# Hadamard transform of the feed-forward input on GpSimd instead of in its weights, norm transposes without TensorE, three slots of keys and values

## The chip, the cores and the metric

The kernel runs on one core of a Trainium2 chip, in float32. A core has five engines that work side by side, each through its own queue of instructions in program order: TensorE (PE, matrix products into PSUM), VectorE (DVE), ScalarE (ACT), GpSimd (POOL) and SyncE (SP), which here issues nearly all DMA transfers. An instruction that waits holds up everything behind it in its queue. The metric is the device time of one execution in microseconds (us): the median of three runs before the change is 2125.62 (2123.35 to 2127.01).

## The reference

One transformer block with modulated norms, 4 sequences of 1024 tokens, 512 features, 16 query heads of 32 that share one key and one value head, and a feed-forward part of width 2048 whose input and inner activations pass a Walsh-Hadamard transform (`fwht`, normalized):

```python
mod = (silu(c) @ wmod).reshape(4, 6, 1, -1)       # sa, ca, ga, sb, cb, gb
ga, gb = sign(ga) * maximum(abs(ga), 0.25), sign(gb) * maximum(abs(gb), 0.25)
h = layernorm(x) * (1 + ca) + sa
x = x + ga * attention(h)                         # causal; q, k, v, o with biases
h = layernorm(x) * (1 + cb) + sb
# feed-forward of h:
u = fwht(h * SU_ug) / SCALE
up   = u @ W_up.T   * (Wscale_ug[:2048] * SCALE)
gate = u @ W_gate.T * (Wscale_ug[2048:] * SCALE)
d = fwht(silu(gate) * up * SU_dp) / SCALE
x = x + gb * (d @ W_down.T * (Wscale_dp * SCALE))
```

## The kernel before

The 4096 tokens form 8 blocks of 512 (two to a sequence), 16 halves of 256 and 32 token tiles of 128. The kernel does not write its instructions in a fixed order: each part (norms, projections, scores, exponentials, attention products, feed-forward, loads) is a generator that yields operations with a cost in microseconds, the keys it reads and writes, and conditions to wait for. A planner (`Flow`) keeps a clock for each engine from these costs, emits the operation that can begin first and, among those within 0.3 us on the same engine, the one of the lowest rank. So each engine's queue order is fixed when the kernel is built, out of the planned costs. The chip then runs each queue in that order and waits where real durations differ from planned ones.

*Attention.* `first_norms` loads a half (2 tiles), takes mean and variance on DVE, the inverse root on POOL (`rstd_op`), normalizes on DVE, and `norm_half` transposes it with eight 128x128 TensorE transposes (L300) into PSUM, from where ACT scales and shifts it into `hT` (L305). `fronts` makes keys, values and queries from `hT` (L271). A `Unit` is one tile of queries by 8 or 16 heads. For each, `scores` (PE, L420), `minima` (DVE, L441), `exps` (ACT, L463), `scales` (ACT, and POOL for every other head of block 0, L487 and L484), `turns` (DVE 32x32 transposes, L502) and `attend` (PE, L529) follow, with two units in flight in the buffer `p`. Keys and values of one whole sequence are kept, so the first block of the next sequence waits until the last one has been attended. `finish` folds the heads (L563) and multiplies by the output weights (L271). `add` multiplies by the gate `ga` and adds `x` on POOL (L593, L594), stores the tile to DRAM (`x2_d`, called x_d in the trace) and takes its statistics.

*Feed-forward.* `second_norms` loads tiles from `x2_d` again, normalizes them, and `norm_half` turns them on TensorE into `bt`. `gate_up` computes gate and up with a two-by-two block scheme of seven products (L905, weights `wa` and `wb` streamed from DRAM), `copies`, `sums` and `multiply` work on them on ACT and DVE (L979, L992, L1008, L1013), and `down` multiplies by the down weights `wd` (L1043). `outputs` adds the result on DVE and POOL (L1070, L1075). A feed-forward block may start once `st.normed` says that all four of its tiles are in `bt` and the four sums T1 to T4 are made (L616). Ranks put attention ahead of `down` and `gate_up`, so the feed-forward of one block fills TensorE beside the attention of the next.

*Preparation.* The Hadamard transforms do not act on activations but on weights. `load_jobs` brings 18 jobs of 1 MB into three buffers in `p`: 6 parts of the modulation weights and 4 each of gate, up and down. `butterflies` does the outer steps on DVE and POOL (L763), `transforms` the inner 128-point transform as TensorE products (L788 to L795) with an ACT copy (L801), and `mixes` (L832) forms the sums of the block scheme, which are stored to `wa_d` and `wb_d`. `hand_over` waits until this is done, frees the buffers and lets `gate_up` begin.

All transfers of the feed-forward are issued on SP in the planned order, with 2 buffers for `wa` and `wb` and 3 for `wd`.

Of the kernel before, what the change touches and what calls it, by code (L numbers as in the profile page):

```python
# [9 lines left out]
F32 = mybir.dt.float32  # L10
# [150 lines left out]
def adaln_block(ctx, tc, x_d, small_d, const_d, wmod_d, qwT_d, kwT_d, vwT_d, vb_d, owT_d, ob_d,  # L161
# [16 lines left out]
    x2_d = dram.tile([B * S, D], F32, name="x2_d")  # L178
    wd_d = dram.tile([NFC, P, D], F32, name="wd_d")
    gates_d = dram.tile([2, B, D], F32, name="gates_d")  # L180
    rows = [slice(HD * j, HD * j + HD) for j in range(4)]

# [3 lines left out]
    xn = {"a": sb("xna", 2, D), "f": sb("xnf", 2, D)}  # L186
    xr, xo = sb("xr", 2, D), sb("xo", 2, D)
# [6 lines left out]
    cg, wgh, qbs = sb("cg", NFC), sb("wgh", NFC), sb("qbs", NDC)  # L194
    scT = sb("scT", NDC, HD)
    kT = sb("kT", S)
    vT = sb("vT", HB)
    vrep = sb("vrep", S // 32, HD)
# [7 lines left out]
    mv = {"a": sb("mva", 2, 2, 2), "f": sb("mvf", NBLK * NT, 2)}  # L206
    rstd = {"a": sb("rstda", 2, 2), "f": sb("rstdf", 2, 2)}
    PB = 8192
    p = sb("p", 2 * PB)
# [3 lines left out]
    oT = sb("oT", 4, H, 32)  # L213
    rden = sb("rden", 4, H)
    aT = sb("aT", NDC, P)
    ga, y, y2 = sb("ga", D), sb("y", 2, D), sb("y2", D)
# [46 lines left out]
    def bk(b):  # L263
        return ("bank", b)
# [21 lines left out]
    def norm_half(which, buf, means, rs, rkey, dst, dkey, scale, bias, need, free):  # L286

        x = xn[buf]
        for j in range(2):
            yield Op("DVE", 0.62, lambda: nc.vector.tensor_scalar(  # L290
                x[:, j, :], x[:, j, :], means[j], rs[:, j:j + 1], ALU.subtract, ALU.mult),
                [rkey], [("xn", buf, j)])
        yield free
        yield banks.have(2)
        bb = banks.take(2)

        def turn():
            for dc in range(NDC):
                for j in range(2):
                    nc.tensor.transpose(ps[:, bb[dc // 2], (dc % 2) * HB + j * P:][:, 0:P],  # L300
                                        x[:, j, dc * P:(dc + 1) * P], ident)
        yield Op("PE", 8 * 0.107 + 0.05, turn, [("xn", buf, 0), ("xn", buf, 1)],
                 [bk(b) for b in bb], mode="full")
        for dc in range(NDC):
            yield Op("ACT", act_cost(HB), lambda: nc.scalar.activation(  # L305
                dst(dc), ps[:, bb[dc // 2], (dc % 2) * HB:][:, 0:HB], AF.Identity,
                bias=bias[:, dc:dc + 1], scale=scale[:, dc:dc + 1]), [bk(bb[dc // 2])] + need, [dkey(dc)])
            if dc % 2:
                banks.give(bb[dc // 2])


    def first_norms(halves):
        for hh in halves:
            i, hf = divmod(hh, 2)
            b = i // BPB

            buf = "f" if hh == 1 else "a"
            x = xn[buf]
            yield lambda: st.fronts >= (hh - 1 if hh > 1 else 0)
            for j in range(2):  # L320
                r = hh * HB + j * P
                yield load(0.25, x[:, j, :], x_d[r:r + P, :], [("xn", buf, j)])
            m = mv["a"][:, hf]
            for j in range(2):
                yield stats_op("a", j, x[:, j, :], m[:, j, :], [("xn", buf, j)], ("mva", hf, j))
            rs = rstd["a"][:, hf, :]
            yield rstd_op(rs, m[:, :, 1], [("mva", hf, 0), ("mva", hf, 1)], ("rstda", hf))
            yield from norm_half("a", buf, [m[:, j, 0:1] for j in range(2)], rs, ("rstda", hf),
                                 lambda dc: hT[:, dc, :], lambda dc: "hT",
                                 modT[:, 1, :, b], modT[:, 0, :, b], ["mod0", "mod1"],  # L330
                                 lambda: st.fronts >= hh)
            st.first_normed = hh + 1

    def fronts(blocks):
        for i in blocks:
            b, t = divmod(i, BPB)
            for hf in range(2):
# [3 lines left out]
                yield lambda: t or st.attended_blocks >= i  # L341
# [37 lines left out]
    class Unit:  # L379
# [11 lines left out]

        def key(self, h):
            return ("p", self.base, h)

    units = []
    for i in range(NBLK):
        heads = 8 if i % BPB or i == 0 else 16
# [744 lines left out]
```

## Time and profile before

The profiled execution took 2121.98 us, of which the span of the program is 2120.1. It reads as follows ("busy" is the time in which an engine has an instruction running; a busy TensorE includes the modelled ends of pipelined products):

| stretch, us from the start | what runs | PE busy | DVE busy | ACT busy | POOL busy | DMA share |
|---|---|---|---|---|---|---|
| 0 to 50 | loads, first norms | 37.51 | 17.34 | 17.29 | 11.00 | 0.72 |
| 50 to 100 | preparation, block 0 of attention | 49.07 | 37.41 | 31.26 | 22.42 | 0.66 |
| 100 to 150 | the same | 45.96 | 42.61 | 31.90 | 36.67 | 0.89 |
| 150 to 200 | the same | 46.71 | 43.31 | 32.00 | 40.60 | 0.35 |
| 250 to 500 | feed-forward beside attention | 236.80 | 162.78 | 143.56 | 17.28 | 0.34 |
| 500 to 1000 | the same | 496.20 | 320.64 | 301.44 | 37.20 | 0.38 |
| 1000 to 1500 | the same | 496.60 | 317.50 | 295.78 | 41.20 | 0.39 |
| 1950 to 2120 | last feed-forward block | 158.71 | 54.63 | 28.67 | 8.50 | 0.46 |

The first gate and up product (L905) starts at 236.6 us; the last feed-forward block starts at 1958 us. The granted TensorE clock is 0.991 of full speed over the span.

### The profile page before, as it was taken

How to read it: one execution, taken by the hardware profiler on the slowest of the kernel's cores; microseconds unless marked ns; L12 is line 12 of the kernel's file. 1: busy time of each engine (PE TensorE's matmuls, PEld its weight loads, DVE VectorE, ACT ScalarE, POOL GpSimd, SP SyncE). 2: the span in 40 equal slices, each digit the busy share in tenths (PEclk: the TensorE clock that was granted, in tenths of full speed). 3: DMA queues.
4: the chain of work that ended last, by engine and by line, in shares of the span. 5: the costliest groups of instructions: out<-in, count | busy, mean ns of one | idle time of the engine just before them, and what ended most of it. 6: DMA issues, size and time to landing. Idle time of an engine off the chain costs nothing.

```text
span 2120.1 us, 41569 instructions
## 1 busy us (share of the span) xinstructions
PE 2056.1 (97%) x16884; PEld 1323.9 (62%) x16884; DVE 1315.7 (62%) x3057; ACT 1172.2 (55%) x2417; POOL 256.6 (12%) x224
## 2 busy tenths in 40 slices
PE   7999899989999999999999999999999999999998
PEld 4545566637766556666666656665766656664774
DVE  3788657774566777763566667763566667764331
ACT  3665556573756666654567565644757565553220
POOL 2467000100000100001100100001100100001000
PEclk9999899998999999999999999999999999999999
DMA  6773433332343434343433444334343444335443
GB/s 241 252 254 110 142 115 118 125 115 66 112 132 110 140 124 131 96 145 98 131 120 122 136 127 133 117 106 131 98 139 100 130 138 132 117 101 161 142 154 121
DMA packets 144599, 280.18 MB, mean 132 GB/s; under 512 B 14092, under 2 KB 44940, under 8 KB 144408
## 3 DMA queue, kind: packets, MB, share of 16 engines
q1 hardware_dynamic: 141384, 274.84, 40.4%
q8 instruction: 133, 2.18, 0.4%
q10 hardware_dynamic: 3024, 2.69, 0.4%
q14 instruction: 58, 0.48, 0.1%
HBM read 241.81 MB, written 35.67 MB: 131 GB/s over the span
## 4 chain that ended last, share of the span: by engine, by line
PE 89%; DVE 3%; issue 2%; DMA 2%; POOL 2%; ACT 1%; SPq 0%; POOLq 0%; ACTq 0%; DVEq 0%
PE ps L905 37%; PE ps L1043 20%; PE ps L271 11%; PE ps L529 9%; PE ps L420 7%; PE ps L563 1%; PE ps L300 1%; DVE p L441 1%; PE ps L794 1%; PE ps L795 1%; POOL p L484 1%; DVE p L502 1%; DMA p<-in_wgT 1%; DMA wd<-wd_d 1%; PE ps L788 0%
## 5 line engine op out<-in xcount | busy, mean ns | idle before, releaser
L905 PE MATMUL ps<-bt,wa 128*128 128x256 f32 x2560 | 607.0, 382 | 6.6 <-issue 4.2
L905 PEld LDWEIGHTS ps<-bt,wa 128*128 128x128 f32 x2560 | 483.5, 191 | 109.2 <-issue 29.2
L1043 PE MATMUL ps<-wd,g 128*128 128x512 f32 x1024 | 480.9, 603 | 6.7 <-DVE g L1018 3.9
L502 DVE STREAM_TRANSPOSE p<-p 128x256 f32<-128x256 f32 (+7 forms) x256 | 347.0, 1368 | 121.6 <-ACT p L487 111.3
L463 ACT ACTIVATE p<-p,nm 128x512 f32<-128x512 f32 (+7 forms) x512 | 390.9, 767 | 34.4 <-DVE nm L441 34.3
L487 ACT ACTIVATE p<-p,rden 128x640 f32<-128x640 f32 (+7 forms) x480 | 347.4, 783 | 25.0 <-DVE rden L467 24.9
L441 DVE CUSTOM_DVE_ANT_0 p<-ps,maskw 128x512 f32<-128x512 f32 (+3 forms) x512 | 277.2, 585 | 105.6 <-PE ps L420 105.1
L992 DVE TENSOR_TENSOR s<-ps,s 128x256 f32<-128x256 f32 x384 | 161.0, 420 | 274.7 <-PE ps L905 205.8
L1043 PEld LDWEIGHTS ps<-wd,g 128*128 128x128 f32 x1024 | 184.7, 190 | 219.0 <-issue 175.7
L905 PE MATMUL ps<-bt,wb 128*128 128x256 f32 x1024 | 271.5, 387 | 0.6 <-DVE s L992 0.5
L905 PEld LDWEIGHTS ps<-bt,wb 128*128 128x128 f32 x1024 | 187.6, 190 | 93.0 <-issue 51.2
L529 PE MATMUL ps<-p,vrep 32*32 32x256 f32 (+1 forms) x8256 | 196.3, 418 | 18.5 <-DVE p L502 7.3
L1008 ACT ACTIVATE th<-s,wgh 128x512 f32<-128x512 f32 x128 | 92.4, 722 | 202.0 <-DVE g L1018 158.0
L420 PE MATMUL ps<-kT,qT 32*128 32x512 f32 (+3 forms) x1536 | 188.6, 533 | 2.9 <-DVE nm L441 2.3
L983 ACT COPY s<-ps 128x256 f32<-128x256 f32 x128 | 47.6, 372 | 254.7 <-PE ps L905 254.7
L593 POOL TENSOR_TENSOR y<-y,ga 128x512 f32<-128x512 f32 x32 | 40.7, 1272 | 1156.6 <-DVE y L576 1088.4
L529 PEld LDWEIGHTS ps<-p,vrep 32*32 32x32 f32 x8256 | 123.4, 104 | 90.5 <-issue 33.7
L441 DVE CUSTOM_DVE_ANT_0 p<-ps,maskw,nm 128x128 f32<-128x128 f32 (+3 forms) x256 | 129.4, 546 | 20.2 <-PE ps L420 20.0
L420 PEld LDWEIGHTS ps<-kT,qT 32*128 32x128 f32 x1536 | 69.5, 183 | 97.8 <-issue 67.4
L539 ACT COPY oT<-ps 128x256 f32<-128x256 f32 (+1 forms) x208 | 75.8, 430 | 90.9 <-PE ps L529 89.7
L271 PE MATMUL ps<-ow,aT 128*128 128x512 f32 x256 | 115.4, 593 | 1.8 <-ACT aT L567 1.8
L271 PE MATMUL ps<-hT,qw 128*128 128x256 f32 x512 | 116.4, 384 | 0.3 <-DVE nm L441 0.3
(99 smaller groups left out, 1585.0 us busy)
## 6 DMA issues: line engine op xcount, KB each, us to landing
wa<-wa_d SPq DMA_DIRECT2D x128, 640.0 KB, 4.7
wd<-wd_d SPq DMA_DIRECT2D x256, 256.0 KB, 2.6
wb<-wb_d SPq DMA_DIRECT2D x128, 256.0 KB, 2.6
xr<-in_x SPq DMA_DIRECT2D x32, 256.0 KB, 2.8
x_d<-xr SPq DMA_DIRECT2D x32, 256.0 KB, 2.1
xnf<-x_d SPq DMA_DIRECT2D x32, 256.0 KB, 3.7
xo<-x_d SPq DMA_DIRECT2D x32, 256.0 KB, 3.9
out<-xo SPq DMA_DIRECT2D x32, 256.0 KB, 2.3
```

What stands on the lines that cost most here:

```text
L271: nc.tensor.matmul(out, l, r, start=(k == 0), stop=(k == len(pairs) - 1))
L420: nc.tensor.matmul(ps[:, bb[j], 0:n], qT[r, c, u.ql * P:(u.ql + 1) * P], kT[r, kb * 512:kb * 512 + n], start=True, stop=True)
L441: yield Op("DVE", 0.245 + 0.00103 * n, lambda: nc.vector.tensor_tensor_reduce(o, ps[:, bb[j], 0:n], m, -1.0, nm[:, slot, 0, j:j + 1] if kb ...
L463: yield Op("ACT", act_cost(u.kmax) + 0.19, lambda: nc.scalar.activation(e, e, AF.Exp, bias=nm[:, slot, u.t, j:j + 1], scale=-1.0, accum_ou ...
L487: yield Op("ACT", act_cost(u.kmax), lambda: nc.scalar.activation(e, e, AF.Copy, scale=r), [("rden", ds, c)], [u.key(h)])
L502: yield Op("DVE", 0.135 + 0.00105 * 2 * u.kmax, lambda: nc.vector.transpose(e, e), [], [u.key(h), u.key(h + 1)])
L529: nc.tensor.matmul(ps[rows[c], bb[g], 0:w], vrep[rows[g], 4 * kt + c, :], pv[rows[g], :, k:k + 32], start=(kt == 0), stop=(kt == nkt - 1))
L539: yield Op("ACT", act_cost(w), lambda: nc.scalar.copy(oT[:, g, u.h0:u.h0 + u.heads, :], ps[:, bb[g], 0:w].rearrange("p (h q) -> p h q", q= ...
L905: nc.tensor.matmul(o, ff[name][:, k % 2, j, c * P:(c + 1) * P], bt[:, t, c, :], start=start and c == 0, stop=stop and c == 1, skip_group_c ...
L992: yield Op("DVE", 0.43, lambda: nc.vector.tensor_add(s[:, j, :], ps[:, bank, half * HB:(half + 1) * HB], s[:, j, :]), [bk(bank)], [sk[j]])
L1008: yield Op("ACT", act_cost(512), lambda: nc.scalar.activation(th, s[:, 0:2, :], AF.Tanh, scale=wgh[:, f:f + 1]), [sk[0], sk[1]], ["th"])
L1043: nc.tensor.matmul(ps[:, acc[j], :], g[:, j * P:(j + 1) * P], ff["wd"][:, m % NWD, :], start=(f == 0), stop=(f == NFC - 1))
```

## The change

The Hadamard transform of the feed-forward's input now acts on the activations. The new `transformed` takes each tile after `add`, normalizes and modulates it with two DVE instructions (rows `sc2r`, `bi2r` spread over the partitions), does nine steps of sums and differences of neighbours on GpSimd (18 instructions of 128x256), transposes 32x32 squares on DVE, and writes the tile with four DMAs (`turn`) to a transposed copy in DRAM, `xTf_d`. `inputs` loads it into `bt` (`turned`). The norms of attention from the third half on take the same way through `xTa_d`, with ACT modulating `hT` in place; the first two halves keep the TensorE transposes. Gate and up weights need no transform: `mixes` works on the raw weights, `butterflies` and `transforms` keep the down weights only. Keys and values have three slots of a block in place of one sequence. `oT` holds 8 heads, so `finish` folds in two steps. On POOL, one head in four instead of two is scaled, in the first three tiles of block 0. The jobs are in another order, and modulation part 5 is the last of them. The modulation gates and the rows `sc2`, `bi2` are made transposed and turned back by TensorE (`turn_back`).

```diff
+    xT_d = {"a": dram.tile([NHALF, D, HB], F32, name="xTa_d"), "f": dram.tile([NHALF, D, HB], F32, name="xTf_d")}
...
+    NKV = 3
+    kv_slot, kv_behind, last_use = {}, [], [-1] * NKV
+    for i, (b, t) in enumerate(order):
+        k = min(range(NKV), key=lambda k: last_use[k])
+        kv_behind.append(last_use[k] + 1)
+        kv_slot[b, t] = k
+        last_use[k] = order.index((b, 1))
...
-    def norm_half(which, buf, means, rs, rkey, dst, dkey, scale, bias, need, free):
...
+    def turn(which, n, x, xk):
+        hh, j = divmod(n, 2)
+        dst = xT_d[which][hh].rearrange("(b q) (j a i) -> j a q b i", q=32, j=2, a=4)[j]
+        for a, r in enumerate(rows):
+            yield load(0.0625, dst[a], x[r, :].rearrange("q (b i) -> q b i", i=32), [("xT", which, n, a)], [xk])
+
+    def turned(which, hh, c, dst, key):
+        return load(0.25, dst, xT_d[which][hh][c * P:(c + 2) * P, :].rearrange("(c p) n -> p c n", p=P), [key],
+                    [("xT", which, n, a) for n in (2 * hh, 2 * hh + 1) for a in range(4)])
...
+                if hh > 1:
+                    yield Op("DVE", 0.67, lambda: nc.vector.transpose(x[:, j, :], x[:, j, :]), [], [(xk, j)])
+                    yield from turn("a", 2 * hh + j, x[:, j, :], (xk, j))
...
-                yield lambda: t or st.attended_blocks >= i
+                yield lambda: st.attended_blocks >= kv_behind[i]
...
-                if u.i == 0 and j % 2:
+                if u.i == 0 and j == 3 and u.ql < 3:
                     yield Op("POOL", 0.3 + 0.0018 * u.kmax, lambda: nc.gpsimd.tensor_scalar(
...
-    def second_norms():
+    def transformed():
+        for n in range(NBLK * NT):
...
+            yield Op("DVE", 0.7, lambda: nc.vector.scalar_tensor_tensor(x, x, m[:, 0:1], sc2r, ALU.subtract, ALU.mult),
+                     ["sc2r", ("mvf", j)], [xk])
+            yield Op("DVE", 0.7, lambda: nc.vector.scalar_tensor_tensor(x, x, rs, bi2r, ALU.mult, ALU.add),
+                     ["bi2r", ("rstdf", j)], [xk])
+            u, w = x, ht
+            for _ in range(9):
+                pairs = u.rearrange("p (n two) -> p two n", two=2)
+                yield Op("POOL", 1.3, lambda: (nc.gpsimd.tensor_add(w[:, 0:D // 2], pairs[:, 0, :], pairs[:, 1, :]),
+                                               nc.gpsimd.tensor_sub(w[:, D // 2:D], pairs[:, 0, :], pairs[:, 1, :])),
+                         [], [xk, "ht"])
+                u, w = w, u
+            yield Op("DVE", 0.67, lambda: nc.vector.transpose(x, ht), ["ht"], [xk])
+            yield from turn("f", n, x, xk)
+            st.added = n + 1
+
+    def inputs():
         for i in range(NBLK):
...
+                yield lambda: st.added >= i * NT + 2 * hf + 2 and st.gated >= i and "mixes" in over
+                for c in (0, 2):
+                    yield turned("f", 2 * i + hf, c, bt[:, c + hf], ("bt", c + hf))
...
-        for _ in range(12):
+        for _ in range(D // P):
             yield lambda: bool(to_fly) and any(tmp_free)
...
-                            nc.tensor.matmul(ps[:, o + j, :], had[:, 0, :], tm[:, j, :], start=True, stop=False)
-                            nc.tensor.matmul(ps[:, o + j, :], had[:, q // 2, :], tm[:, 2 + j, :],
-                                             start=False, stop=True)
...
-            yield lambda: len(to_mix) > 1
+            yield lambda: len(to_mix) > 1 and st.first_normed > 1
...
-        yield lambda: "transforms" in over and "mixes" in over
+        yield lambda: "transforms" in over and "mixes" in over and "mods done" in over
```

## The prediction

> **What bounds the kernel now.** I read the busy shares and the chain of waits first, to find the engine that sets the time.
>
> ```profile
> PE 2056.1 (97%) x16884; PEld 1323.9 (62%) x16884; DVE 1315.7 (62%) x3057; ACT 1172.2 (55%) x2417; POOL 256.6 (12%) x224
> ...
> PE 89%; DVE 3%; issue 2%; DMA 2%; POOL 2%; ACT 1%; SPq 0%; POOLq 0%; ACTq 0%; DVEq 0%
> ```
>
> TensorE has hardly any idle time, and 89% of the chain is TensorE itself. Work taken off TensorE therefore counts in full, as long as its queue never waits for what replaces it. Next I read the chain by time, because the average hides that the first 236 us (before the first L905) are another stage:
>
> ```profile
> 62.37 0.87 PE ps L300 x8
> ...
> 78.69 1.06 PE ps L794 x2
> 79.75 0.86 PE ps L795 x2
> ...
> 100.11 2.39 POOL tmp L763
> ...
> 103.77 2.70 POOL p L484 x2
> ...
> 186.18 4.08 POOL p L484 x2
> ...
> 2020.66 6.04 PE ps L905 x28
> ```
>
> Columns are start and length. Between 88 and 190 us the chain changes between POOL, DVE and TensorE; POOL is busy 40.60 of the 50 us from 150 on. So the preparation is set by POOL and DVE, with TensorE close behind. From 500 us on TensorE leaves only about 3.5 us of each 500 idle. The last two rows I use are prices: eight transposes take 0.87 us, a 512-column product (two records) 0.86 us, and 28 records of L905 take 6.04 us, that is 0.431 us for a product of 256 columns.
>
> **What goes from TensorE.** I priced both programs' TensorE queues with such rows. Before holds 1967 us of products, 183 of them ahead of the first L905. After holds 1889, 136 ahead. What goes: 64 Hadamard products of 0.86 us (55 us), all in the preparation, and 240 transposes of 0.109 us (26 us), 200 of which (22 us) come after it. What comes: 16 products that turn rows back, and other products for the modulation, some 4 us, in the preparation.
>
> In the feed-forward stage, from the first L905 on, 1784 us of products become 1753. These 31 us are the 22 of transposes, and 9 of attention of block 1 (a unit and some scores) that the new order puts ahead of the first L905. TensorE is the bound there, so I take **-31 us**.
>
> **The preparation.** On POOL, 6 butterflies (2.6 us) and 20 scalings (1.3 us) go, about 41 us, and four Hadamard transforms of block 0 come. DVE loses 10 butterflies of 1.6 us; ACT loses 16 copies of 1.01 us. But a gate or up buffer is now held from its load until its parts are stored, not freed after the first butterflies. One round of a gate and an up job is a load (6.6 us), S1 on POOL (2.9), three sums on DVE (4 to 5) and the stores (8 to 12 us for 3.7 MB at the 250 to 290 GB/s of these slices): some 25 us. Four rounds from about 33 us on, behind the first down job whose butterfly stands ahead of S1 on POOL, end near 150; the last jobs are a down and modulation part 5, whose product stands in TensorE's queue ahead of the last unit of block 0, near 165. Eleven us of products and the gate's small DVE steps put the last output product of block 0 near 183.
>
> From there the chain to the first L905 is: L576 0.7, two POOL instructions 2.6, statistics 0.9, inverse root 1.0, two DVE instructions of 0.69, the transform 13.8 (below), transpose 0.7, four DMAs to DRAM 3.8 (2.1 to landing as x_d<-xr, and the issues), load 3, first sum 0.7, gaps 1: 29.6 us. That gives 213, and I take 215 in place of 236: **-21 us**. Bounds: 190 if the jobs pack better, 240 if the stores crowd the queues.
>
> **The transform on POOL.** No 256-wide POOL instruction is in the trace. The rows of two lengths give a line:
>
> ```profile
> L763 POOL TENSOR_TENSOR tmp<-p x12: 2334/2364/3401, 23.1 to 196.8; 128x1024 f32<-128x1024 f32 x12
> ...
> L593 POOL TENSOR_TENSOR y<-y,ga x32: 1262/1272/1282, 111.5 to 1946.9; 128x512 f32<-128x512 f32 x32
> ```
>
> Minimum, median and maximum in ns. (2334 - 1262) / 512 = 2.09 ns an element and 190 ns fixed, so 726 ns for 256. Nine steps of two, each step waiting 0.08 us for the one before (the gap from L593 to L594), make **13.8 us** a tile, 442 us in all. POOL has the room: 12% becomes some 30%.
>
> Here the Trainium skill speaks against the change. Its GPSIMD Engine Reference ("Performance versus the Vector engine") has two-input elementwise work about twice as slow on GpSimd as on VectorE and says to use VectorE. The rows agree (2.1 against L763's 1.15 ns an element on DVE), and by that rule the same instructions would take some 230 us on DVE instead of 442 on POOL; but neither engine is the bound, and what decides is the wait. The same page ("Performance pitfalls for Q7 kernels") puts a step of over 8 bytes at 2.9 instead of 1.9 cycles an element. The pairs step by exactly 8 bytes, so the price should stay; if it did not, the tile would cost about 20 us. No row here has such a step. I take 13.8 and keep 20 as the upper end, 13 (no gaps) as the lower.
>
> **The wait it adds.** The planner costs nine steps at 1.3 = 11.7 us, 0.2 of latency, and POOL needs 13.8 plus collisions. The DVE transpose behind it stands in DVE's queue where the planned end is, with minima, sums and products of the feed-forward behind it, and TensorE waits for those. Late by about 2 us, 28 times after the preparation. How much reaches TensorE no row shows; DVE has 36% idle time, and L905 seldom waits for it (idle ahead of it for L992 is 0.5 us in all). From nothing to all of it (0 to 56 us), I take 0.4: **+22 us**.
>
> **Collisions.** DVE rows show what they are:
>
> ```profile
> L1010 DVE SCALAR_TENSOR_TENSOR th<-th,s x128: 646/691/1315, 245.0 to 2081.0; 128x512 f32<-128x512 f32 x128
> ...
> L763 DVE TENSOR_TENSOR tmp<-p x20: 1177/1220/3385, 21.5 to 203.8; 128x1024 f32<-128x1024 f32 x20
> ```
>
> The maximum of L763 is the minimum and nearly one POOL instruction (2.2 us). The skill's page SBUF — State Buffer ("Who interferes with whom") says why: a DVE instruction with two SBUF inputs, or in a two-port mode, and a GpSimd instruction lock each other out for a whole instruction. By the median rows of the feed-forward the price is zero, since POOL is nearly idle there. By the rule, some 400 such DVE instructions (L1010, L1013, L616, the two new ones, the norms) meet a POOL that is busy 22% of the time, each losing half of 0.73 us: 32 us of DVE, a fifth of it on TensorE's path: **+6** (0 to 20).
>
> **The rest of the edits.** DVE gains 60 transposes of 0.70 and 32 times two instructions of 0.69 and loses 32 of 0.64: +66 us, under TensorE's cover; ACT loses 31 us of L305. SP's queue grows from 766 to 1059 issues of 0.3 to 0.4 us, 100 us in a queue that mostly waits. The 240 writes move 128-byte pieces; the trace has no such write. 128-byte reads took 14 ns a packet, 0.45 us for 512 packets on 16 DMA engines; the skill (DMA: Bandwidth & Descriptors, first table) has under 512 bytes as read-modify-write, and at twice the 28 ns that 512-byte packets took a write would be 1.8 us, 7 a tile. The weights' loads queue behind, with a chunk (7.8 us) of lead: +2 (0 to 15).
>
> SP's wait for the tile before its store exists already (SPq behind L594: 149.5 us, 30 times) and now stands behind the transpose too. The third slot removes the wait for the last unit at a sequence's end: the one visible stall there is L529 behind L502 at 479 us, 7.3 us: **-6**. At the first boundary after it, 19 us of products lie between the last output product of block 1 and the feed-forward that needs it, against a chain of 29.6; before, 21.6 against a shorter chain left about 3 us: **+8**. At the other boundaries 33 to 120 us cover it, at the last one 41. Folding in two steps adds 37 changes of TensorE's tiling at 0.1 us: +4.
>
> Sum: -31 - 21 - 6 + 22 + 6 + 2 + 8 + 4 = **-16 us** on the profiled execution's 2122, that is 2106. The median stands 3.6 above that execution, so 2109.
>
> **Rivals.** (A) The preparation packs to 190 and the planned places hide the waits: -31 - 46 - 6 + 20 = -63, 2062. For it: POOL loses its queue of butterflies and scalings, and L905 hardly waits for DVE. Against: the buffers held until stored, and modulation part 5 in TensorE's queue.
>
> (B) **Slower**: DVE stands behind the transform. If a tile takes 20 us (step price, or locks against DVE's rows as in the preparation, where L763 averages 1608 ns instead of 1220), the transpose is 8 us late; with half of it reaching TensorE, 28 x 4 = 112 in place of 22, and with 6 more at the boundaries the sum is +80: 2205. It decides from about 16 us a tile, where 28 x 4 x 0.4 = 45 uses up the gain; at 17 to 18 us it gives 2140 to 2160, its likeliest range. For it: L763's stretched rows. Against: L593's maximum of 1282 in the feed-forward.
>
> (C) The transposes and products leave, and waits take exactly their place: 2126.
>
> **Chances.** Forecast (2090 to 2119) 0.42, A 0.17, B 0.32, C 0.09. Under 0.2% (4 us) cannot be told from no change. Faster 0.58, same 0.09, slower 0.33. The range 2055 to 2162 takes in A and B's likeliest part.
>
> **What would show it.** POOL instructions of 128x256 at 0.73 us; the first L905 near 215 us; 38 us of wait or less ahead of TensorE in the middle slices; DVE's transposes of `ht` waiting some 2 us for POOL. A POOL median near 1.1 us, or waits of 8 us there, makes B true; a first L905 after 240 would break the preparation's sum.

## The result, and the profile after

The changed kernel takes 2128.9 us (median, 2122.6 to 2133.0) against 2123.6 us for the kernel before, both over 20 runs on one chip: a ratio of 1.003, 95% interval 1.0021 to 1.0040. It is slower by about 5 us; another order of the same instructions moves either kernel by more than that (runs 8, 15 and 18), so the sign of these 5 us says little. What is to be explained is the forecast gain of 16 us that is not there. The profiled execution took 2131.84 us, its span 2130.0, that is 9.9 us more than the profiled span before.

The busy shares and the chain by engine, against the first two lines that the prediction shows:

```profile
PE 2013.5 (95%) x16560; PEld 1288.0 (60%) x16560; DVE 1370.6 (64%) x3146; ACT 1146.1 (54%) x2437; POOL 580.0 (27%) x806
...
PE 82%; DVE 5%; issue 3%; DMA 3%; POOL 3%; ACT 2%; SPq 1%; POOLq 0%; DVEq 0%; ACTq 0%
```

TensorE was busy 42.6 us less, and the kernel still took longer: 7% of the chain moved from TensorE to DVE (2%) and, by 1% each, to POOL, DMA, ACT, issue and the queue of SyncE. So the work did leave, and idle time took its place. To find where, I split the span at the moment from which the feed-forward can go on (the T1 products of the first `first()`; the B11 products ahead of them can run earlier), and summed TensorE's records and the gaps between them (some 6 us of each span lie behind TensorE's last record):

| | feed-forward goes on at | TensorE busy before that | rest of the span | busy in it | gaps in it |
|---|---|---|---|---|---|
| before | 238.4 | 209.5 | 1881.7 | 1846.6 | 28.6 |
| changed | 242.7 | 184.2 | 1887.3 | 1829.2 | 51.6 |

The preparation ends 4.3 us later, though TensorE is busy 25 us less in it. The rest is 5.6 us longer: 17.4 us of work gone, 23.0 us of gaps come. Windows of the preparation, first two of the kernel before, then the same of the changed one (columns: window, length, busy us of PE, PEld, DVE, ACT, POOL, granted TensorE clock, DMA share, GB/s):

```profile
50.00:100.00 50.00, 49.07 (x303) 26.81 (x303) 37.41 (x105) 31.26 (x91) 22.42 (x18) 1.00 0.66 223
100.00:150.00 50.00, 45.96 (x400) 24.21 (x399) 42.61 (x73) 31.90 (x81) 36.67 (x24) 1.00 0.89 291
```

```profile
50.00:100.00 50.00, 39.44 (x316) 20.92 (x316) 28.45 (x91) 33.43 (x110) 17.62 (x15) 0.76 1.02 312
100.00:150.00 50.00, 40.62 (x414) 23.64 (x414) 39.55 (x80) 28.12 (x73) 34.59 (x28) 0.86 0.78 244
150.00:200.00 50.00, 42.20 (x438) 22.67 (x438) 45.60 (x93) 31.14 (x69) 27.71 (x34) 0.90 0.72 206
```

From 50 to 100 us the DMA engines are full, and TensorE stands idle for 10.6 us; its longest waits there are 3.5 us for a butterfly on GpSimd and 3.3 us for a modulation weight from DRAM. With the gaps the granted clock falls from 1.00 to 0.76 (over the whole preparation it is 0.83, before 0.97), so what is left of its work takes longer: the prediction counted 136 us of products ahead of the first L977, and TensorE was busy 184 us with them (183 and 209.5 before). From 150 us on VectorE is the fullest (45.60 of 50; 43.31 before).

In the feed-forward stage, what TensorE waited for after 245 us (waiting line, releaser, us, times, longest):

```profile
PE ps L977 <- DVE bt L694: 11.1, 2, 7.8
PE ps L582 <- issue: 10.2, 10, 2.9
PE ps L1115 <- DVE g L1090: 6.0, 9, 0.9
PE ps L618 <- DVE g L1090: 5.8, 6, 1.1
PE ps L1115 <- DMA wd<-wd_d: 3.8, 6, 0.9
PE ps L582 <- DVE p L554: 3.1, 1, 3.1
...
PE ps L618 <- DVE rden L519: 1.8, 2, 1.0
...
PE ps L618 <- ACT oT L595: 0.8, 1, 0.8
```

There is no single large stall. L977 behind L694 is the chain of a block's inputs at two boundaries. L618 is new: the second fold of a tile. The transform itself is seen in the groups of the tile `ht` (minimum, median, maximum in ns):

```profile
L679 POOL TENSOR_TENSOR ht<-xr x160: 608/612/1473, 140.4 to 1947.3; 128x256 f32<-128x256 f32 x160
...
L683 DVE STREAM_TRANSPOSE xr<-ht x32: 668/710/714, 171.3 to 1948.5; 128x512 f32<-128x512 f32 x32
its engine sat idle before it (us, times) until:
...
  POOL ht L680: 21.5, 13
```

A GpSimd instruction takes 612 ns in the median where 726 were forecast, and VectorE's transposes waited for GpSimd 21.5 us in all, in 13 of 32 cases.

### The profile page after: what moved, and what is told of

Its sections match the earlier page's. It is cut to its first block, busy times and chain, and to the rows that moved or that the text cites. A ratio compares the mean times of both kernels' runs of the same rounds, so it can differ in the third digit from the quotient of the medians.

```text
span 2130.0 us, 42155 instructions
## 1 busy us (share of the span) xinstructions
PE 2013.5 (95%) x16560; PEld 1288.0 (60%) x16560; DVE 1370.6 (64%) x3146; ACT 1146.1 (54%) x2437; POOL 580.0 (27%) x806
## 4 chain that ended last, share of the span: by engine, by line
PE 82%; DVE 5%; issue 3%; DMA 3%; POOL 3%; ACT 2%; SPq 1%; POOLq 0%; DVEq 0%; ACTq 0%
PE ps L977 37%; PE ps L1115 17%; PE ps L294 9%; PE ps L582 8%; PE ps L472 6%; PE ps L618 2%; DVE p L554 1%; SPq L283 1%; DVE p L493 1%; ACT p L539 1%; PE ps L867 1%; DMA p<-in_wgT 1%; DMA bi2r<-rows_d 1%; PE ps L870 1%; POOL ht L680 0%
## 5 line engine op out<-in xcount | busy, mean ns | idle before, releaser
L977 PE MATMUL ps<-bt,wa 128*128 128x256 f32 x2560 | 614.4, 385 | 16.0 <-DVE bt L694 12.7
L977 PEld LDWEIGHTS ps<-bt,wa 128*128 128x128 f32 x2560 | 484.5, 192 | 126.6 <-issue 29.8
L1115 PE MATMUL ps<-wd,g 128*128 128x512 f32 x1024 | 482.6, 606 | 11.4 <-DVE g L1090 6.0
L554 DVE STREAM_TRANSPOSE p<-p 128x256 f32<-128x256 f32 (+7 forms) x256 | 344.9, 1364 | 91.3 <-ACT p L539 89.1
L539 ACT ACTIVATE p<-p,rden 128x128 f32<-128x128 f32 (+7 forms) x500 | 356.5, 775 | 36.4 <-DVE rden L519 36.2
L1115 PEld LDWEIGHTS ps<-wd,g 128*128 128x128 f32 x1024 | 185.4, 190 | 231.3 <-issue 182.0
L977 PE MATMUL ps<-bt,wb 128*128 128x256 f32 x1024 | 270.8, 387 | 1.1 <-DVE s L1064 1.1
L977 PEld LDWEIGHTS ps<-bt,wb 128*128 128x128 f32 x1024 | 189.0, 190 | 93.5 <-issue 53.0
L582 PE MATMUL ps<-p,vrep 32*32 32x256 f32 (+1 forms) x8256 | 199.9, 424 | 37.0 <-DVE rden L519 18.0
L650 POOL TENSOR_TENSOR y<-y,ga 128x512 f32<-128x512 f32 x32 | 41.6, 1301 | 703.9 <-DVE y L633 666.3
L472 PE MATMUL ps<-kT,qT 32*128 32x512 f32 (+3 forms) x1536 | 194.7, 536 | 3.5 <-ACT oT L595 1.9
L582 PEld LDWEIGHTS ps<-p,vrep 32*32 32x32 f32 x8256 | 123.8, 105 | 109.3 <-issue 40.2
L1051 ACT COPY s<-ps 128x512 f32<-128x512 f32 x128 | 74.9, 585 | 142.5 <-PE ps L977 130.0
L1147 POOL TENSOR_TENSOR xo<-xo,y 128x512 f32<-128x512 f32 x32 | 41.6, 1300 | 390.1 <-DVE y L1142 390.1
L679 POOL TENSOR_TENSOR ht<-xr 128x256 f32<-128x256 f32 x160 | 102.8, 642 | 133.7 <-DVE xr L674 120.3
L472 PEld LDWEIGHTS ps<-kT,qT 32*128 32x128 f32 x1536 | 72.4, 184 | 94.5 <-issue 67.2
```

Of the source, the lines that this page charges most:

```text
L472: nc.tensor.matmul(ps[:, bb[j], 0:n], qT[r, c, u.ql * P:(u.ql + 1) * P], kT[r, u.kv[kb] * TB:u.kv[kb] * TB + n], start=True, stop=True)
L539: yield Op("ACT", act_cost(u.kmax), lambda: nc.scalar.activation(e, e, AF.Copy, scale=r), [("rden", ds, c)], [u.key(h)])
L554: yield Op("DVE", 0.135 + 0.00105 * 2 * u.kmax, lambda: nc.vector.transpose(e, e), [], [u.key(h), u.key(h + 1)])
L582: nc.tensor.matmul(ps[rows[c], bb[g], 0:w], vrep[rows[g], v0 + c, :], pv[rows[g], :, k:k + 32], start=(kt == 0), stop=(kt == nkt - 1))
L679: yield Op("POOL", 1.3, lambda: (nc.gpsimd.tensor_add(w[:, 0:D // 2], pairs[:, 0, :], pairs[:, 1, :]), nc.gpsimd.tensor_sub(w[:, D // 2:D] ...
L977: nc.tensor.matmul(o, ff[name][:, k % 2, j, c * P:(c + 1) * P], bt[:, t, c, :], start=start and c == 0, stop=stop and c == 1, skip_group_c ...
```

## The experiments

The edits are to the changed kernel unless told otherwise. "Goes on" and "gaps after" are the first and the last column of the table above; the wait just before the moment at which the feed-forward goes on is not in the gaps. Any edit changes planned costs or conditions, and the planner then puts the whole queues in another order, so each time holds some chance of the order; runs 8, 15 and 18 measure it.

| run | median us | ratio to before, 95% | goes on | gaps after |
|---|---|---|---|---|
| changed kernel | 2128.9 | 1.0030 (1.0021-1.0040) | 242.7 | 51.6 |
| 1 products back | 2167.7 | 1.0213 (1.0197-1.0229) | 274.2 | 49.5 |
| 2 one step | 2110.5 | 0.9943 (0.9926-0.9960) | 217.1 | 44.4 |
| 3 two slots | 2165.3 | 1.0185 (1.0152-1.0219) | 244.3 | 73.5 |
| 4 two slots, one fold | 2135.0 | 1.0058 (1.0040-1.0076) | 236.7 | 54.7 |
| 5 one step in block 0 | 2119.4 | 0.9989 (0.9976-1.0003) | 214.8 | 51.0 |
| 6 three slots, one fold | 2110.7 | 0.9944 (0.9923-0.9965) | 239.2 | 36.4 |
| 7 norms on TensorE | 2125.7 | 1.0018 (1.0008-1.0027) | 236.9 | 41.9 |
| 8 window 0.4 | 2161.4 | 1.0197 (1.0176-1.0217) | 243.1 | 71.1 |
| 9 two buffers | 2124.6 | 1.0012 (1.0000-1.0024) | 250.4 | 46.3 |
| 10 transform first | 2146.8 | 1.0112 (1.0090-1.0135) | 260.9 | 48.0 |
| 11 one fold, window 0.4 | 2133.6 | 1.0045 (1.0030-1.0061) | 247.1 | 45.0 |
| 12 whole fold, unguarded | 2102.4 | 0.9910 (0.9884-0.9936) | 233.1 | 38.8 |
| 13 whole fold, guarded | 2102.0 | 0.9889 (0.9868-0.9909) | 239.2 | 37.6 |
| 14 whole fold, from PSUM | 2091.4 | 0.9850 (0.9832-0.9867) | 235.3 | 29.8 |
| 15 before, window 0.4 | 2134.0 | 1.0051 (1.0037-1.0064) | 238.5 | 36.8 |
| 16 block 0 on VectorE | 2145.8 | 1.0113 (1.0088-1.0138) | 251.8 | 50.6 |
| 17 as 14, window 0.3 | 2116.4 | 0.9972 (0.9961-0.9983) | 247.8 | 40.2 |
| 18 changed, window 0.15 | 2151.6 | 1.0127 (1.0087-1.0166) | 240.2 | 63.9 |

### The preparation: runs 1, 2, 5, 10 and 16

Run 1 puts back the product work that was taken out of the preparation:

```diff
             (a, gs), (_, us) = to_mix.popleft(), to_mix.popleft()
+            for gu in (gs, us):
+                for q in range(2):
+                    yield banks.have(1)
+                    o, = banks.take(1)
+                    def idle_products():
+                        for j in range(4):
+                            nc.tensor.matmul(ps[:, o, :], had[:, 0, :], raws[gu][:, j, :],
+                                             start=(j == 0), stop=(j == 3))
+                    yield Op("PE", mm(512, 4), idle_products, [("raw", gu), "had0"], [bk(o)], mode="full")
+                    banks.give(o)
```

> The changed kernel, with 64 products of 128x512 put back on TensorE in the preparation: for each of the eight gate and up blocks eight products of the raw block with the Hadamard matrix, whose results nobody reads, ahead of the mixes. That is the product work that the change took out of the preparation (64 times 0.857 us = 55 us). Theory 1 (the preparation is not bound by TensorE, so what was taken out there bought nothing, and idle TensorE ran at a lower granted clock): time 2120 to 2138, first gate-and-up product between 235 and 250 us, granted clock of the preparation near 0.95 instead of 0.83. Rival (TensorE's work is worth its length there, as the forecast's rounds have it, and the gain was lost elsewhere): first gate-and-up product at 275 us or later, time 2165 or more.

The feed-forward goes on 31.5 us later (its first product starts at 270.1, just short of the rival's 275), and the time lies in the rival's band. So theory 1 fell: the removed products were not free. They were not worth their length either: of 55 us put back 23.5 were absorbed, and the clock came back with them (run 1's window, to be held against 0.76 above):

```profile
50.00:100.00 50.00, 49.12 (x276) 29.30 (x275) 26.49 (x79) 30.99 (x97) 13.41 (x14) 0.97 0.79 232
```

The products stand ahead of the mixes in the same stream and so hold the weights' buffers longer, which is in the 31.5. But something worth some 30 us must have come into the preparation in their place. Run 2 leaves out eight of the nine steps everywhere, run 5 in the four tiles of block 0 alone:

```diff
-            for _ in range(9):
+            for _ in range(1):                      # run 2
+            for _ in range(9 if n >= NT else 1):    # run 5
```

> The changed kernel with one step of the transform on GpSimd instead of nine (this leaves out most of the transform): 16 of 18 GpSimd operations of each tile gone, some 10 us a tile. If the transform's length is what costs (waits of VectorE behind it, the chain to the first feed-forward block, collisions[...]): 2095 to 2108, that is 21 to 34 us better than the changed kernel. If the gain was lost elsewhere (preparation held by buffers and DMA, many small waits of the new attention tail): only the chain ahead of the first block gets shorter, by 10 to 20 us there, and the whole is 2112 to 2124.

> The changed kernel with one step of the transform instead of nine for the four tiles of block 0 only (this leaves out most of their transform); all other tiles keep nine. Theory A (the transform costs in the preparation, where GpSimd has butterflies and mixes to do besides, and little elsewhere): first gate-and-up product between 203 and 212 us, as with one step everywhere (206.6), and the whole within 4 us of that run, 2108 to 2116. Rival B (the transform costs beside the feed-forward, through VectorE's waits and the order of the work): first product near 207 too, but 10 us or more above the run with one step everywhere: 2121 or more.

In both the feed-forward goes on 26 to 28 us earlier, at 217.1 and 214.8 us. This is no chance of the order: the changed kernel goes on at 242.7, 243.1 and 240.2 in its three orders. So the four transforms of block 0 are what took the preparation's gain. For the whole time neither run fits one theory cleanly: 2110.5 lies between the two bands of run 2, and 2119.4 between the bands of A and B.

Beside the feed-forward the transform shows at two boundaries. This is TensorE's wait there, first in run 5, after its feed-forward has gone on; the changed kernel's is the first line of the list above, and run 2 has none:

```profile
PE ps L977 <- DVE bt L694: 12.0, 2, 8.1
```

The gaps say the same: 44.4 us with one step everywhere, 51.0 with nine steps outside block 0, 51.6 in the changed kernel. The whole of this is worth 9 us between runs 2 and 5, which is under the chance of the order.

How the four transforms cost 26 us is seen on GpSimd's timeline of the changed kernel, between the last output product of block 0 (its L633 begins at 198.5) and the feed-forward:

```profile
205.59 0.61 POOL L680 TENSOR_TENSOR ht<-xr 128x256 f32<-128x256 f32 x1
206.16 1.27 POOL L650 TENSOR_TENSOR y<-y,ga 128x512 f32<-128x512 f32 x1
207.39 0.61 POOL L679 TENSOR_TENSOR xr<-ht 128x256 f32<-128x256 f32 x1
...
209.79 1.26 POOL L651 TENSOR_TENSOR xr<-xr,y 128x512 f32<-128x512 f32 x1
...
213.42 0.23 POOL L305 TENSOR_SCALAR rstdf<-mvf 128x1 f32<-128x1 f32 x1
...
220.43 0.85 POOL L679 TENSOR_TENSOR ht<-xr 128x256 f32<-128x256 f32 x1 [5.12 <-DVE xr L674]
```

The last tile's gate multiplication (L650), residual (L651) and inverse root (L305) stand in GpSimd's queue among the steps of the tile before it. Its own transform begins at 220.4, 22 us after L633. From L633 (the addition of the output bias, just behind the last output product) to the feed-forward it is 44 us; in runs 2 and 5 it is 25 us, and there L633 itself is 6 to 8 us earlier.

Runs 10 and 16 ask whether it is the order, or GpSimd's slowness. Run 10 gives the inputs' stream precedence in the preparation; run 16 puts block 0's steps on VectorE:

```diff
-(3.5, transformed)
+(early(2.12, 3.5), transformed)                     # run 10
+                e = nc.vector if n < NT else nc.gpsimd    # run 16, planned at 0.8 us a step
```

> The changed kernel with the stream of the feed-forward's inputs (norm, transform, transposes) planned ahead of attention's minima, scales and transposes until the first block is attended, instead of behind them; the same instructions in another order. Theory A1 (the transform of block 0 is late because it stands behind other work on VectorE and GpSimd: in the changed kernel the first tile's result waited from 156.5 to 171 us for VectorE, and the next tile could not begin): feed-forward products go on without a wait from 218 to 231 us instead of 242.8, the whole 2118 to 2126. Rival A2 (GpSimd's own work is too long there whatever the order, 48 us of steps beside 58 us of other work): 238 us or later, the whole within 5 us of the changed kernel or worse.

> The changed kernel with the nine steps of block 0's four tiles on VectorE instead of GpSimd (72 operations of 128x256). If GpSimd's slowness holds the preparation: the feed-forward goes on without a wait by 230 us, and the whole is 2118 to 2126. If the sum of work on VectorE and GpSimd holds it (VectorE is busy for more than 80% of the stretch from 100 to 200 us already): 240 us or later, and the whole 2129 or more.

Both made it later, 260.9 and 251.8. In run 10 the first two transforms ended earlier (139 and 182 us instead of 156 and 194), but the work that they passed was late: the L633 of the last two tiles moved from 170.7 and 198.5 to 186.2 and 233.4. In run 16 VectorE became the bound:

```profile
100.00:150.00 50.00, 37.16 (x400) 21.61 (x397) 45.90 (x86) 28.97 (x73) 28.22 (x16) 0.92 0.81 256
150.00:200.00 50.00, 33.80 (x270) 17.44 (x270) 45.01 (x103) 22.40 (x50) 8.16 (x6) 0.81 0.67 197
200.00:250.00 50.00, 34.49 (x412) 21.91 (x412) 43.90 (x132) 35.79 (x74) 4.30 (x6) 0.67 0.26 60
```

VectorE is busy for 88 to 92% of these windows, TensorE for 68 to 74%, and from 150 us on GpSimd for 16% and less. The same instruction took 420 ns in the median on VectorE, against 612 on GpSimd, so the steps were shorter there and the stretch still longer. So GpSimd's speed alone is not the cause, and this other order was no cure; only two of many placements were tried, and in neither did the stretch take up the steps (four times 12 us on GpSimd) without delay.

### The split fold and the third slot: runs 3, 4, 6, 9 and 11

```diff
-    NKV = 3
+    NKV = 2                                        # runs 3, 4
-    oT = sb("oT", 4, H // 2, 32)
+    oT = sb("oT", 4, H, 32)                        # runs 4, 6, 11: one fold of 16 heads
-                for c in range(2):
+                for c in range(NDC):
-            if half == 0:
-                continue
+    oT = sb("oT", 2, 4, H // 2, 32)                # run 9: two folds, two buffers
```

> The changed kernel with two slots of keys and values instead of three. The forecast priced the third slot at 6 us: 2133 to 2137. If the third slot only moves the wait elsewhere: within 3 us of the changed kernel, 2126 to 2132.

> The kernel of the run with two slots, and the fold of 16 heads at once as in the kernel before (the room for the larger buffer comes from the third slot). Theory 2 (the split fold adds a wait for the copies of the second half, and changes of tiling, in each of 32 tiles): 8 to 20 us faster than the run with two slots alone. Rival (the split costs the 4 us priced in the forecast or less): within 4 us of it.

> The changed kernel with three slots and the fold of all 16 heads at once, as in the kernel before. The 4 KB a partition that this takes come from the output bias and the shift ahead of the transform, in whose place rows of other tiles are read: the bias and the shift are left out of the result, the operations stay. Theory 2 (the split fold costs in every tile, by holding four PSUM banks until the first half is folded and by changes of tiling): 10 to 30 us below the changed kernel, 2099 to 2119, as it was 30 us with two slots. Rival (the 30 us were the two slots' own trouble, and the split costs the 4 us of the forecast): 2122 to 2129.

> The kernel of the run with three slots and one fold (output bias and shift left out, rows of other tiles read in their place), but folded in two halves as in the changed kernel, each half with a buffer of its own, so that the copies of a half no longer wait until the half before is folded. Theory 2a (the wait for the one buffer of eight heads, and the four PSUM banks held meanwhile, is what the split costs): within 6 us of the run with one fold, 2104 to 2117. Theory 2b (the second fold's own instructions and its change of tiling cost): near the changed kernel, 2122 to 2131.

> The kernel of the run with three slots and one fold, with the planner's tie window at 0.4 us, to stand beside the changed kernel at 0.4 us (2161). If the split fold's cost is more than chance of the order: 10 to 35 us below that, 2126 to 2151. If what the fold gained at 0.3 us was chance: within 8 us of 2161, or above.

Runs 6, 9 and 11 leave the output bias, the shift ahead of the transform and their few loads out, so their times stand for the instructions only; run 4 is complete. One fold is faster each time: by 30 us with two slots (run 4 against 3), 18 us with three (run 6), 28 us at the window of 0.4 (run 11 against 8). Each single difference is of the size of chance, but all have one sign, and the trace has the term itself. After 245 us the waits of L618 in the three orders of the changed kernel (window 0.3, runs 8 and 18) are 8.7, 8.8 and 7.5 us of gaps ahead of TensorE, where the one fold of runs 6 and 11 has none. The fold's records also take longer in two parts. Busy us, mean ns and idle us before it, in the changed kernel, in run 6 (where it is L616) and in run 9 (L620):

```profile
L618 PE MATMUL ps<-oT,fold 128*32 128x128 f32 x1024 | 42.6, 283 | 8.7 <-DVE g L1090 5.8 <-DVE rden L519 1.8 <-ACT oT L595 0.8
L616 PE MATMUL ps<-oT,fold 128*32 128x128 f32 x1024 | 35.4, 280 | 0.0
L620 PE MATMUL ps<-oT,fold 128*32 128x128 f32 x1024 | 41.9, 282 | 1.2 <-ACT oT L597 1.2
```

So 7 us of records and 9 us of waits, some 16 us, are seen at the fold itself. Who waited for it after 245 us, in the changed kernel and in run 6:

```profile
  ACT aT L622: 39.0, 28
  ACT oT L595: 3.3, 3
```

```profile
  ACT aT L620: 23.6, 18
```

ACT waits for 39.0 us instead of 23.6, since each tile has two folds and two copies behind them, and copies of `oT` now wait for a fold. With a buffer for each half (run 9) the waits at the fold are all but gone and its records stay; the time falls only to 2124.6, but its preparation ended at 250.4. The rest of the span is 1887.3 us in the changed kernel, 1880.5 in run 9 and 1871.6 in run 6: some 7 us for the buffer and 9 for the second fold, at one order each.

The third slot: two slots cost 36 us with the split fold (run 3), six times the forecast, and 24 us with one fold (run 4 against 6). The sign is the same twice, but neither can be told from chance (window 0.4 alone moved 32 us), so its size stays open.

### Norms through DRAM: run 7

```diff
-                if hh > 1:            # transposes by VectorE and DRAM
+                if hh >= NHALF:       # never: TensorE for all halves
```

> The changed kernel with the normalised tiles of attention transposed on TensorE for all sixteen halves, as it does for the first two, instead of by VectorE and through DRAM. It puts back 14 x 8 transposes, some 10 us of TensorE work, and takes out 28 transposes on VectorE, 112 small writes and 28 loads. Theory 3 (the way through DRAM delays what it feeds: small packets, requests to be issued, loads that land late): 2118 to 2127, the added work more than paid back. Rival (it waits for nobody, and moving the transposes off TensorE is worth its length): 2136 to 2142.

2125.7, inside theory 3's band. Putting 10 us of transposes back on TensorE made the kernel faster by 3 us: busy time after the preparation rose by 8.3 us, the gaps fell by 9.7, and the preparation was 5.8 us shorter. In this order, what the way through DRAM took off TensorE it gave back as waiting. The 3 us are within chance, and a gain of 10 us would be too; that the move is worth its length is not shown.

### Chance of the order: runs 8, 15 and 18

```diff
-    SLACK = 0.3
+    SLACK = 0.4      # run 8; run 15: the same in the kernel before
+    SLACK = 0.15     # run 18
```

> The changed kernel with the planner's tie window at 0.4 us instead of 0.3, nothing else: the same instructions in another order. It is the measure of chance in all these comparisons. If the order that the planner happens on matters little: 2124 to 2134. If it decides differences of this size: 10 us or more away from 2129, to either side.

> The kernel before with the planner's tie window at 0.4 us instead of 0.3, nothing else. If chance of the order is as large in this kernel as in the changed one: 10 us or more away from 2123. If the kernel before is insensitive: within 6 us of it, and then the changed kernel's 30 us at the same window are its own: its streams have more places where one late piece of work holds the rest.

> The changed kernel at the tie window 0.15 us, nothing else. If the window is only chance and made the gain of the version before: 2095 to 2110. If the changed kernel stays where it is: 2122 to 2140.

The same instructions in another order moved the changed kernel by 32 and 23 us, the kernel before by 11. The order at 0.3 is the best of the three tried for the changed kernel, and run 18 is slower than either of its expectations. At 0.4 in both kernels the changed one is 27 us slower. In run 8 one wait of 11.6 us of L582 for L554 came up, with 20.1 us for that pair in all instead of 3.1; that such a stall comes from the place where the planner put a late piece is likely, not shown. A difference of under 20 us in the whole time between two orders is therefore no evidence by itself.

### Versions that keep the fold whole: runs 12, 13, 14 and 17

```diff
-    xn, xr, xo = sb("xn", 2, D), sb("xr", 2, D), sb("xo", 2, D)
+    xn, xr, xo = sb("xn", 1, D), sb("xr", 2, D), sb("xo", 2, D)
-    ga, y, y2 = sb("ga", D), sb("y", D), sb("y2", D)
+    ga, y = sb("ga", D), sb("y", D)
...
-nc.vector.tensor_mul(y2, ps[:, acc[j], :], ff["gb"])
-nc.gpsimd.tensor_add(x, x, y2)
+nc.vector.tensor_mul(y, ps[:, acc[j], :], ff["gb"])                        # runs 12, 13
+nc.gpsimd.tensor_add(x, x, y)
+nc.vector.tensor_mul(ps[:, acc[j], :], ps[:, acc[j], :], ff["gb"])         # runs 14, 17
+nc.vector.tensor_add(x, x, ps[:, acc[j], :])
```

> A complete version: the changed kernel with the fold of 16 heads at once. Its 4 KB come from one tile buffer instead of two for the norms of attention (the first half-tiles use room that is free in the preparation) and from sharing the buffer between the attention output and the feed-forward output; the inputs' stream is planned early as in the run before last, and the tie window is 0.2 us. If the split fold and the late transforms are what ate the gain: 2085 to 2103, faster than both kernels. If not: 2115 or more.

> The changed kernel with the fold of 16 heads at once, complete. The 4 KB come from one tile buffer instead of two for the norms of attention and from one buffer shared by the attention output and the feed-forward output, each of which now waits until the other has been added; tie window 0.15 us. If the split fold is a main loss, and the wait for the shared buffer small: 2092 to 2110, faster than both kernels. If guarding the buffer costs what the fold gains: 2118 or more.

> As the run beside it, but the feed-forward output has no buffer: VectorE multiplies it by the gate in its PSUM bank and adds the residual from there (two VectorE operations a tile instead of one on VectorE and one on GpSimd). It takes the wait for the shared buffer away and adds some 22 us of VectorE work in all. If VectorE has room beside the feed-forward: 2085 to 2108. If VectorE's work delays the gates' products: 10 us or more above the run beside it.

> The complete version with the whole fold and the output from PSUM, at the tie window of the changed kernel, 0.3 us. If its gain is its own: 2093 to 2112. If it was the window's: 2118 or more.

All four have the one fold of 16 heads, and take attention's norms tile by tile. The window is 0.2 us in run 12, which also plans the inputs' stream early as run 10 does, 0.15 in runs 13 and 14, and 0.3 in run 17. In run 12 nothing kept the two users of the shared buffer apart, so some attention rows are replaced by feed-forward rows; its time stands for the instructions only. In run 13 each user takes `y` only after the other's sum is planned. Run 14 is faster than both kernels: 0.985 of the kernel before. Its waits of TensorE after 245 us, the first five:

```profile
PE ps L1120 <- DVE g L1095: 9.3, 14, 1.1
PE ps L590 <- issue: 8.0, 14, 1.6
PE ps L590 <- DVE p L562: 1.8, 2, 1.6
PE ps L590 <- DVE nm L501: 1.7, 1, 1.7
PE ps L982 <- DVE s L1069: 1.5, 3, 1.0
```

The fold is gone from the list, and the gaps are 29.8 us, as in the kernel before, with 31 us less work than there after the preparation (1815.4 against 1846.6). Its last block also has no GpSimd instruction between the down products and the store. Run 17 says how much of this is the order: at the window of the changed kernel the same version takes 2116.4, so 25 of its 37.5 us on the changed kernel are the choice of the window, and 12.5 us are its own at that window, between the two bands of the expectation and under the 20 us of chance. At 0.15 the same comparison gives 60 us (run 18). Both have the same sign; the size is not settled.

## Why the prediction was wrong

The forecast was 2109, the time 2129. By its own steps:

- **The preparation, -21: this is the step that failed.** It came out at +4. The sum named four transforms on GpSimd against 41 us of butterflies and scalings that leave, but put only the last tile's transform into the chain and the last output product at 183 us. Measured: 198.5, and 44 us of chain instead of 29.6. Without eight of the nine steps in block 0 the feed-forward goes on at 217 and 215 (runs 2 and 5). What was left out is that four transforms are one serial stream on engines which the attention of block 0 and the mixes fill. That 215 is also the forecast's figure is luck: the forecast has 13.8 us of transform in it, and without eight steps (12.3 us) the same sum says 201 to 203. So about half of the miss of 28 us is the transforms beyond the one that was priced, and the other half, some 14 us, was missing in the rest of the sum: in runs 2 and 5 L633 is at 192 and 190 instead of 183, and the chain takes 25 us instead of 17. The sum had no term for the granted clock, which is 0.91 over run 2's preparation; whether that makes these 14 us was not tested.
- **-31 for TensorE's work after the preparation:** busy time fell by 17.4. The products of L977, L1115, L582 and L472 are as many as before and took 1762 us instead of 1744 over the whole span, at a granted clock of 0.974 instead of 0.991, and the folds 42.6 instead of 34.6.
- **The wait for the transform, +22: too high.** VectorE's transposes waited 18.4 us in all after 245 us, ten times, and of TensorE only 0.7 us of weight loads stood behind them. A GpSimd step took 612 ns instead of 726.
- **Collisions, +6: they are there.** The medians hide them (485 ns for L1013 before and for L1085 now); the means show them. Busy us and mean ns, two lines before and the same two now:

```profile
L1013 DVE SCALAR_TENSOR_TENSOR g<-th,cg,s 128x256 f32<-128x256 f32 x128 | 63.6, 497 | 4.5
L616 DVE TENSOR_TENSOR bt<-bt 128x512 f32<-128x512 f32 x32 | 20.6, 685 | 6.6 <-ACT bt L305 6.4
L1085 DVE SCALAR_TENSOR_TENSOR g<-th,cg,s 128x256 f32<-128x256 f32 x128 | 68.2, 533 | 4.5
L694 DVE TENSOR_TENSOR bt<-bt 128x512 f32<-128x512 f32 x32 | 26.5, 864 | 13.3 <-DMA bt<-xTf_d 13.2
```

After 245 us the 27 of L1085 that overlap a GpSimd instruction take 711 ns, the 101 others 485; for L694 it is 18 at 1002 against 10 at 686, for L1082 29 at 847 against 99 at 681. L1090, the same operation with one input in PSUM, is not stretched: 473 and 472 ns. That fits the rule of the Trainium skill's page SBUF — State Buffer ("Who interferes with whom"), on which the term rests: a VectorE instruction with two inputs in SBUF contends with a GpSimd one that reads SBUF. In all it is 17 us of VectorE (32 were priced), 6 of them in L694, which TensorE waits for at the boundaries; how much reached the time was not measured alone.
- **The split fold, +4: too low.** It costs 18 to 30 us in three pairs of runs, of which some 16 are seen at the fold: 9 of waits and 7 of its own records.
- **Boundaries, +8:** right. L977 waited for L694 7.8 and 3.3 us at two boundaries.
- **Third slot, -6:** the sign agrees with run 3; the size is open. **DMA, +2:** TensorE's wait for `wd` rose from 2.5 to 3.8 us. The small writes landed in 2.6 us in the median, and the packets of 128 bytes took 13 ns each in the median (14 for the reads before); no price of a read-modify-write shows. But in run 7 the norms' way through DRAM won nothing that shows.

The terms after the preparation sum to +5, and the stage came out at +5.6, by errors that cancel. Rival B had the right side with the wrong mechanism: a tile took 12 us, and VectorE stood behind it for 18.4 us in all, not 8 us a tile. Rival C, 2126, is nearest: the products leave, and waits take their place. What it did not name are the places: the transforms of block 0, and the second fold.

## What to carry to other kernels

Work moved off the bounding engine must be priced in every stage in which it runs, in the queues that it enters there; an engine that is 12% busy over the whole span can be 81% busy in the stage whose end matters (GpSimd before the change, 40.60 of the 50 us from 150 on). A buffer halved to make room can cost more than it seems, in waits and in pieces of work that are smaller and more: try to free the room elsewhere first, as run 14 does. A collision of two engines is read from means, or from the records that overlap, not from medians. Where a planner orders the queues, try a few orders of both kernels before a difference of one per cent is believed.

## What was not expected of the hardware

Idle time of TensorE was followed by slower products, so it cost twice. In run 2 TensorE waits 9.43 us at the first T1 product; records that took 379 ns before the gap take up to 794 ns after it, and it is only after 222 us that they shorten:

```profile
199.63 7.17 PE L294 MATMUL ps<-hT,qw 128*128 128x256 f32 x32
206.64 1.03 PE L977 MATMUL ps<-bt,wa 128*128 128x256 f32 x4
217.09 2.07 PE L977 MATMUL ps<-bt,wa 128*128 128x256 f32 x4 [9.43 <-DVE bt L694]
```

Four records in 1.03 us before the gap, four in 2.07 after it. The Trainium skill's TensorE: Matmul & The Clock Gate ("Part 1: The HAM clock gate") states half the clock after an idle window of about 3.4 us, until about 3.4 us of busy time; here the granted clock is 0.50 from 213 to 223 us, so the slow stretch lasted some 6 us after the gap. Over the preparation, busy time times granted clock is 184.2 x 0.83 = 153 us, before 209.5 x 0.97 = 203: a rough estimate, 50 us less, near the 47 us of products that were taken out. That accounts for TensorE being only 25 us less busy.

The 256-wide GpSimd instruction reads its pairs 8 bytes apart and takes 612 ns in the median, a little less than half of the 1272 ns of a contiguous 512-wide one (L650): neither a fixed part nor a price for the step shows.
